# Selective scan: 512-column scans with a carried start value become 1024-column scans with a standing zero decay between the two halves

## The chip, the cores and the metric

The kernel runs on one core of a Trainium2 chip. The metric is the device time of one launch in microseconds (us); lower is better.

## The reference, cut to what matters

The reference is a chain of four layers on a tensor of 2 images with 128 channels of 64x64 pixels. Layers 0 to 2 (attention, a snake convolution, three convolution steps) are not touched. Layer 3 runs a Mamba block over each image in four directions (rows and columns, each forwards and backwards). Its core is a linear recurrence over 4096 positions, for 256 inner channels times 16 states:

```
dA = jnp.exp(dt[..., None] * A)
dBu = dt[..., None] * Bm[:, :, None, :] * xh[..., None]
def step(h, inp):
    dA_t, dBu_t = inp
    h = dA_t * h + dBu_t
    return (h, h)
_, hs = lax.scan(step, h0, (dA.transpose(1, 0, 2, 3), dBu.transpose(1, 0, 2, 3)))
y = jnp.einsum('lbdn,bln->bld', hs, Cm)
```

`dA` is the decay, `dBu` the input term (the "product with B"), `hs` the states, and `y` sums the states times C.

## The kernel before, in words

**Tiling.** Layer 3 (`layer3`, from line 1230) cuts each sequence of 4096 into 8 chunks of `BLK` = 512 positions. Two images, four directions and 8 chunks give 64 blocks. In a block the 256 x 16 states are worked off as 8 *groups* of 512 states: half `hf` (0, 1) by quarter of the states `ng` (0 to 3). The text calls them g0 to g7 (g0 to g3 are `hf` 0, g4 to g7 are `hf` 1). A group has a tile `db` of 128 partitions x 4 columns `q` x 512 positions, which holds first the product with B, then (in place) the states, then (in place) the states times C.

**The loop.** The main loop runs over the groups, k = 8i + slot, with the names "block i, slot s". The order on each engine is written by hand (`tc.manual_schedule()`), and every engine works off its own list in that order; between engines there are semaphores only. One turn of the loop with number k does:

- TensorE: `weights(k+2)` (line 1501), at the start of the turn: a matmul that spreads the four rows of B that this group needs over the partitions, into the PSUM tile `pbc` (pool `psb`, 2 buffers).
- ScalarE: `expo` (1544) computes one decay tile `da` of 512 columns (pool `psd`, 3 buffers of PSUM), two tiles ahead of the scan that uses it. For some columns it also runs an activation on a single column (1550) which adds the decayed last state of the previous chunk to the first product, so that the scan may start at 0.0. Those are columns q = 2, 3, and all four where VectorE makes no product; the other scans take the last state `hl` as their start value.
- VectorE: `scan` (1558) four times, 512 columns each; then `db_dve(k+1)` (1522), the product with B for the first `ND[hf][ng]` of the 512 positions, read from `pbc`.
- ScalarE: `keep(k-1)` (1563) saves the last states.
- GpSimd: `cmul(k-1)` (1568) multiplies states by C, and `db_pool(k+2)` (1531) makes the product with B for the positions from `ND` on, from copies of B in SBUF.
- TensorE: `sums(k-2)` (1574, 1576) folds the states into `y`; at `ng` 0 it first adds the direct term (1574).

`ND` is (512, 0, 176, 512) for `hf` 0 and (512, 512, 0, 512) for `hf` 1. So g1 and g6 have their product wholly from GpSimd, and g2 has 336 of 512 positions from it.

**The front of the next block** is spread over the slots of this one. At the end of each turn come `front_pe`, `front_act` and `front_pool`, and then `sums(k-2)`:

| slot | TensorE | ScalarE |
|---|---|---|
| 0 | `xproj` (1428) | `xproj_copy` (two copies, 1434, 1436) |
| 1 | `delta` (1455) | `softplus` of half 0 (1461 to 1464) |
| 2 | `sum_parts` of half 0 (1469) | `softplus` of half 1, `sum_copy` (1472) |
| 3 | `sum_parts` of half 1, `xproj_rest` (1446, 1447) | `sum_copy`, `rest_copy` (1450) |
| 4 | `zproj` (1416) | `zproj_silu` (1422, with two table loads) |
| 5 | `sums`, `project` of the block before (1593, 1595), then `conv` of half 0 (1404) | |
| 6 | `conv` of half 1 (1404) | `finish` of the block before (1601, 1603 or 1606) |
| 7 | | `conv_silu` (1409, with two table loads) |

All these TensorE results go through the PSUM pool `psm` with two buffers, so a matmul waits until the result two places earlier in that pool has been read. In slots 2 and 6 VectorE also gates `y` (1585). In 13 of the 64 blocks a layer norm of 512 columns for later use is spread over the same slots (`ln_mean` and others, lines 1326 to 1362).

The eight PSUM banks go to: `psd` 3, `psb` 2, `psy` 1 (for `y`), `psm` 2.

Of the kernel before, what the change touches and what calls it, by code (L numbers as in the profile page):

```python
# [1229 lines left out]
def layer3(g, I, out):  # L1230
# [5 lines left out]
    nc, tc = g.nc, g.tc  # L1236
    NJ = 4

    ND = ((BLK, 0, 176, BLK), (BLK, BLK, 0, BLK))
    NNG = N_STATE // NJ  # L1240
    HB = 1
    HC = 3
    with ExitStack() as ctx:
        a = ctx.enter_context(tc.tile_pool(name="l3a", bufs=1))
        dr = ctx.enter_context(tc.tile_pool(name="l3dr", bufs=2, space=bass.MemoryType.DRAM))
        psd = ctx.enter_context(tc.tile_pool(name="l3psd", bufs=3, space=PSUM))
        psb = ctx.enter_context(tc.tile_pool(name="l3psb", bufs=2, space=PSUM))
        psy = ctx.enter_context(tc.tile_pool(name="l3psy", bufs=1, space=PSUM))
        psm = ctx.enter_context(tc.tile_pool(name="l3psm", bufs=2, space=PSUM))

# [64 lines left out]
        xt = a.tile([P, L + 2 * HC], F32, name="xt")  # L1315
        N = {}
        NFIRST = 3


        def ln_tile():  # L1320

            return psd.tile([P, BLK], F32, name="da")

        def ln_mean(b, k):
            N[k, "mean"] = ln_tile()
            nc.tensor.matmul(N[k, "mean"], onesm, interior(g, b, k * RB, RB), start=True, stop=True)

        def ln_less(b, k):
# [10 lines left out]
            nc.scalar.activation(N[k, "sq"], N[k, "xc"], AF.Square)  # L1339

        def ln_var(b, k):
            N[k, "var"] = ln_tile()
            nc.tensor.matmul(N[k, "var"], onesm, N[k, "sq"], start=True, stop=True)


        def ln_log(b, k):
            nc.scalar.activation(N[k, "sq"], N[k, "var"], AF.Ln, bias=g.eps5)
# [37 lines left out]
        def reverse(i):  # L1385
            b, nd, _ = blocks[i]
            return dirs[b][nd][2]
# [91 lines left out]
        def spread_store(i, hf):  # L1479

            S[i]["dx", hf] = dr.tile([P, 2, BLK], F32, name="dx")
            nc.sync.dma_start(S[i]["dx", hf], S[i].pop(("dd", hf)))

        def spread_load(i, hf):
            s_ = S[i]
            dx = s_.pop(("dx", hf))
            dd4 = d4.tile([P, 2, 4, BLK], F32, name="dd4")
            for x in range(2):
                src = dx[:, x, :].rearrange("(q c) t -> c q t", c=32)
                for j in range(NJ):  # L1490
                    nc.sync.dma_start(dd4[32 * j : 32 * j + 32, x], src)
            s_["d4", hf] = dd4

        def weights(k):

            i, hf, ng = groups[k]
            G[k] = {}
            if ND[hf][ng] == 0:
                return
            pb = psb.tile([P, BLK], F32, name="pbc")  # L1500
            nc.tensor.matmul(pb, sel[:, ng].rearrange("p j c -> p (j c)"), S[i]["bc"], start=True, stop=True)  # L1501
            G[k]["pb"] = pb
# [8 lines left out]
                nc.sync.dma_start(t[32 * j : 32 * j + 32], S[i]["bx"][r0 + j].partition_broadcast(32))  # L1511

        def db_tile(k):
            if "db" not in G[k]:
                G[k]["db"] = wk.tile([P, 4, BLK], F32, name="db")
            return G[k]["db"]

        def db_dve(k):
            i, hf, ng = groups[k]
            n = ND[hf][ng]  # L1520
            if n:
                nc.vector.tensor_tensor(  # L1522
                    db_tile(k)[:, :, :n], G[k].pop("pb")[:, :n].unsqueeze(1).to_broadcast([P, 4, n]),
                    S[i]["d4", hf][:, 1, :, :n], ALU.mult,
                )
# [7 lines left out]
                    S[i]["d4", hf][:, 1, :, n:], ALU.mult,  # L1533
                )

        def carried(k, q):

            i, hf, ng = groups[k]
            return i % NBLK > 0 and (q >= 2 or ND[hf][ng] == 0)

        def expo(k, q):
            i, hf, ng = groups[k]
            da = psd.tile([P, BLK], F32, name="da")
            nc.scalar.activation(da, S[i]["d4", hf][:, 0, q, :], AF.Exp, scale=am[:, hf, q, ng : ng + 1])  # L1544
            G[k]["da", q] = da
            if carried(k, q):

                first = BLK - 1 if reverse(i) else 0
                b0 = G[k]["db"][:, q, first : first + 1]
                nc.scalar.activation(b0, da[:, first : first + 1], AF.Identity, bias=b0, scale=hl[:, hf, ng, q, :])  # L1550

        def scan(k, q):
            i, hf, ng = groups[k]
            d0, d1 = G[k].pop(("da", q)), G[k]["db"][:, q, :]
            if reverse(i):
                d0, d1 = d0[:, ::-1], d1[:, ::-1]
            zero = i % NBLK == 0 or carried(k, q)
            nc.vector.tensor_tensor_scan(d1, d0, d1, 0.0 if zero else hl[:, hf, ng, q, :], ALU.mult, ALU.add)  # L1558

        def keep(k):  # L1560
            i, hf, ng = groups[k]
# [75 lines left out]
        def transfers(i, slot):  # L1637
            if i < NBK:
                if slot == 1:
                    bc_store(i)  # L1640
                elif slot == 4:
                    spread_store(i, 0)
                elif slot == 5:
                    spread_load(i, 0)
                    spread_store(i, 1)
            if slot == 0 and i - 1 < NBK:
                spread_load(i - 1, 1)
            for x, ahead in (("b", 4), ("c", 1)):
                j, ng = divmod(8 * (i - 1) + slot + ahead, 8)
                if ng < NNG and 0 < j < NBK:  # L1650
                    copies(j, x, ng)
# [21 lines left out]
        def front_pool(i, slot):  # L1673
            if i < NBK:
                if slot in (3, 4):
                    spread(i, slot - 3)
# [9 lines left out]
        with tc.manual_schedule():  # L1686
# [4 lines left out]
            nc.vector.memset(xt[:, HC + L :], 0.0)  # L1691
            nc.vector.memset(xn[:, HB - 1, HW - HC :], 0.0)
            nc.vector.memset(xn[:, HB + HW, :HC], 0.0)
            units = [(k, q) for k in range(len(groups)) for q in range(4)]
            AHEAD = 2

            for k in range(NFIRST):
                ln_mean(0, k)
            for k in range(NFIRST):
# [34 lines left out]
            for ng in range(NNG):  # L1734
                copies(0, "b", ng)
                copies(0, "c", ng)
            for k in range(2):
                weights(k)
            db_dve(0)
            db_pool(0)  # L1740
            front_pe(0, 4)
            front_act(0, 4)
            front_pe(0, 5)
            front_pe(0, 6)
            for u in range(AHEAD):
                expo(*units[u])
            front_act(0, 7)
            db_pool(1)
            for k in range(len(groups) + 7):
                i, slot = divmod(k, 8)  # L1750
                live = k < len(groups)
                more = k + 1 < len(groups)
                ended = 1 <= k <= len(groups)
                transfers(i + 1, slot)
                if k + 2 < len(groups):
                    weights(k + 2)
                norm = next_norm(i)
                for q in range(4):
                    if slot == 6 and q == 3 and 1 <= i <= NBK:
                        finish(i - 1)  # L1760
                    if norm and slot == 2 and q == 3:
                        ln_log(*norm)
                    if q == 0 and ended:
                        keep(k - 1)
                    if 4 * k + q + AHEAD < len(units):
                        expo(*units[4 * k + q + AHEAD])
                    if norm and q == 0:
                        if slot == 0:
                            ln_mean(*norm)
                        elif slot == 2:  # L1770
                            ln_var(*norm)
                    if live:
                        scan(k, q)

                    for j, hf in (((k - 6) // 8, 0), ((k - 10) // 8, 1)):
                        if q == 1 and 8 * j + 6 + 4 * hf == k and 0 <= j < NBK:
                            gate(j, hf)
                if norm and slot == 0:
                    ln_less(*norm)
                if more:  # L1780
                    db_dve(k + 1)
                if ended:
                    cmul(k - 1)
                if k + 2 < len(groups):
                    db_pool(k + 2)

                if slot == 5 and 0 <= k - 2 < len(groups):
                    sums(k - 2)
                if slot == 5 and 1 <= i <= NBK:
                    project(i - 1)  # L1790
                front_pe(i + 1, slot)
                front_act(i + 1, slot)
                front_pool(i + 1, slot)
                if norm:
                    if slot == 1:
                        ln_square(*norm)
                    elif slot == 3:
                        ln_root(*norm)
                    elif slot == 5:
                        ln_scale(*norm)  # L1800
                    elif slot == 6:
                        ln_store(*norm)
                if live:

                    if slot == 6 and 0 < i % (4 * NBLK) <= NBLK // 2:
                        for n in range(2):
                            turn(blocks[i][0], 2 * (i % (4 * NBLK) - 1) + n)

                if slot != 5 and 0 <= k - 2 < len(groups):
                    sums(k - 2)  # L1810


@with_exitstack
# [157 lines left out]
```

## Time and profile before

| quantity | value |
|---|---|
| median of 3 runs | 5609.23 us (5607.43 to 5609.56) |
| the profiled execution's own time | 5610.11 us |
| its span, first to last instruction | 5608.3 us |
| first and last scan of layer 3 start at | 2309.3 and 5593.2 us |
| busy share of the span: TensorE, VectorE, ScalarE, GpSimd | 84%, 81%, 73%, 65% |
| mean granted TensorE clock | 0.877 |

The page of the profile gives busy time of each engine (PE is TensorE, PEld its weight loads, DVE is VectorE, ACT is ScalarE, POOL is GpSimd), groups of equal instructions with their busy time, the mean duration of one in ns and the idle time ahead of them with what ended it ("<-"). A timeline lists an engine's instructions in order: start in us, duration in us, engine, line, operation, output <- input, "x" the count of merged ones, and in brackets the idle time just before. Instructions of an engine overlap a little at their ends, so four of 1.20 us can take 4.57 us. Layer 3 is the stretch from 2309 us to the end: 64 blocks in some 3284 us, 51.3 us each.

### The profile page before, as it was taken

The numbers are of one execution on the slowest core, as the hardware profiler recorded it, in microseconds if no ns is written. First come the engines' busy times: TensorE is split into PE (matmuls) and PEld (weight loads), VectorE is DVE, ScalarE is ACT, GpSimd is POOL, SyncE is SP. The second block draws the span as 40 slices with busy tenths as digits, with TensorE's granted clock in tenths as the row PEclk, the third lists the DMA queues.
The fourth block names the chain that finished last, engine by engine and source line by source line (L and its number), as shares of the span: only waits on it lengthen the run. The fifth ranks groups of instructions, "written<-read, shape, count | busy, mean of one in ns | idle before, by whom it ended". The sixth has DMA issues, their size and how long they took to land.

```text
span 5608.3 us, 54471 instructions
## 1 busy us (share of the span) xinstructions
PE 4731.0 (84%) x17062; PEld 1757.8 (31%) x17062; DVE 4537.0 (81%) x4232; ACT 4086.5 (73%) x6282; POOL 3661.7 (65%) x1197
## 2 busy tenths in 40 slices
PE   6999999899788699777788887878888888877786
PEld 3444444344344244222222222222222222222221
DVE  6566555552144998699999999999999999999998
ACT  3999999500255311698888888888888888888886
POOL 6222222100100311599999999999999999999999
PEclk8999999999899899888888888888878787888887
DMA  4111111300375000465565556556555655565554
GB/s 155 38 46 46 31 31 38 62 1 1 76 128 83 27 0 0 104 143 129 129 141 137 135 126 144 129 129 148 140 133 128 144 134 131 130 147 131 134 137 106
DMA packets 334569, 554.27 MB, mean 99 GB/s; under 512 B 69264, under 2 KB 115872, under 8 KB 334080
## 3 DMA queue, kind: packets, MB, share of 16 engines
q1 hardware_dynamic: 331136, 547.17, 41.2%
q10 hardware_dynamic: 3136, 3.56, 0.3%
q8 instruction: 135, 2.21, 0.2%
q14 instruction: 162, 1.33, 0.1%
HBM read 461.40 MB, written 89.13 MB: 98 GB/s over the span
## 4 chain that ended last, share of the span: by engine, by line
DVE 45%; PE 35%; ACT 11%; issue 5%; DMA 2%; POOL 1%; SPq 1%; DVEq 0%; ACTq 0%; POOLq 0%
DVE db L1558 30%; DVE db L1522 11%; PE ps L312 8%; PE acc L328 8%; PE m L1112 5%; PE m L600 5%; ACT da L1544 4%; PE acd L846 2%; ACT db L1550 1%; DVE gt L1585 1%; PE m L560 1%; ACT L1409 1%; ACT u L1409 1%; PE pf L809 1%; DMA hats<-pos 1%
## 5 line engine op out<-in xcount | busy, mean ns | idle before, releaser
L1568 POOL TENSOR_TENSOR db<-db,c 128x2048 f32<-128x2048 f32 x512 | 2314.0, 4535 | 48.3 <-ACT hl L1563 32.7
L1544 ACT ACTIVATE da<-dd,am 128x512 f32<-128x512 f32 x2048 | 1398.6, 687 | 300.4 <-DVE db L1558 281.6
L1558 DVE TENSOR_TENSOR_SCAN db<-da,db 128x512 f32<-128x512 f32 x1376 | 1585.2, 1204 | 36.3 <-ACT db L1550 28.1
L318 ACT ACTIVATE e<-ps 128x1536 f16<-128x1536 f32 (+1 forms) x683 | 919.0, 1624 | 7.9 <-PE ps L312 7.9
L1558 DVE TENSOR_TENSOR_SCAN db<-da,hl,db 128x512 f32<-128x512 f32 x672 | 825.9, 1271 | 41.6 <-POOL db L1531 2.6
L1522 DVE TENSOR_TENSOR db<-pbc,dd 128x2048 f32<-128x2048 f32 (+1 forms) x384 | 781.3, 2035 | 32.1 <-DMA dd<-dx 32.1
L1531 POOL TENSOR_TENSOR db<-b,dd 128x2048 f32<-128x2048 f32 (+1 forms) x192 | 773.5, 4029 | 12.7 <-DMA b<-bx 12.7
L1576 PE MATMUL py<-db,fold 128*32 128x512 f32 x4096 | 615.6, 687 | 153.2 <-POOL db L1568 153.1
L312 PE MATMUL ps<-q 128*128 128x512 f16 x2048 | 554.0, 379 | 4.3 <-DVE flag L260 2.7
L328 PE MATMUL acc<-e,v 128*128 128x512 f16 x2048 | 553.7, 379 | 0.1
L346 POOL TENSOR_TENSOR parts<-parts 32x512 f32<-32x512 f32 x64 | 80.6, 1259 | 707.5 <-DVE parts L345 707.5
L1550 ACT ACTIVATE db<-da,db,hl 128x1 f32<-128x1 f32 x1120 | 394.0, 352 | 146.7 <-DVE db L1522 103.2
L339 DVE RECIPROCAL rec<-acc 32x512 f32<-32x512 f32 x64 | 214.9, 3358 | 257.9 <-PE acc L328 248.3
L1112 PE MATMUL m<-v,u 128*128 128x512 f32 x864 | 379.3, 602 | 41.8 <-DVE v L1055 40.9
L1469 PE MATMUL pm<-dd,ident 128*128 128x512 f32 x512 | 359.7, 841 | 2.5 <-ACT dd L1462 2.5
L1428 PE MATMUL pm<-u,wxp 128*72 128x512 f32 x256 | 196.7, 913 | 141.0 <-ACT u L1409 141.0
L1501 PE MATMUL pbc<-bc,sel 64*128 64x512 f32 x384 | 208.3, 542 | 123.6 <-DVE db L1522 122.8
L312 PEld LDWEIGHTS <-q 128*128 128x128 f16 x2048 | 197.7, 97 | 278.5 <-issue 103.6
L328 PEld LDWEIGHTS <-v 128*128 128x128 bf16 x2048 | 199.3, 97 | 248.8 <-issue 10.2
L600 PE MATMUL m<-comb,w 64*128 64x512 f32 (+4 forms) x1296 | 269.9, 575 | 0.0
L720 POOL TENSOR_SCALAR yt<-y 32x512 f32<-32x512 f32 x8 | 18.1, 2268 | 380.8 <-DVE y L711 380.4
L1576 PEld LDWEIGHTS py<-db,fold 128*32 128x32 f32 x4096 | 90.6, 114 | 553.2 <-issue 306.7
(324 smaller groups left out, 6563.4 us busy)
## 6 DMA issues: line engine op xcount, KB each, us to landing
dd<-dx SPq DMA_DIRECT2D x1024, 256.0 KB, 6.5
dx<-dd SPq DMA_DIRECT2D x128, 512.0 KB, 5.4
c<-bx SPq DMA_DIRECT2D x1024, 64.0 KB, 2.1
hats<-pos SPq DMA_DIRECT2D x136, 256.0 KB, 9.8
b<-bx SPq DMA_DIRECT2D x512, 64.0 KB, 4.6
piece<-qd SPq DMA_DIRECT2D x128, 128.0 KB, 2.8
piece<-kd SPq DMA_DIRECT2D x112, 128.0 KB, 2.7
w<-in_conv0T SPq DMA_DIRECT2D x18, 288.0 KB, 8.5
```

The lines of the kernel that those rows point to most:

```text
L312: nc.tensor.matmul(ps[:, i, :], t[:, 1, kb * P : (kb + 1) * P], t[:, 0, qb * BLK : (qb + 1) * BLK], start=True, stop=True,)
L318: nc.scalar.activation(e[:, :n, :], ps[:, :n, :], AF.Exp, scale=1.0 / UP**2)
L328: nc.tensor.matmul(acc, v3[b][:, kb, h, :], e[:, i, :], start=(kb == 0), stop=(kb == NS - 1))
L600: yield lambda q=q, dy=dy, src=src, i0=i0, i1=i1: nc.tensor.matmul(m[:, i0 * NF : i1 * NF], w[half, dy, q, x, :], src, start=(dy == KC and ...
L1112: nc.tensor.matmul(m[x], weights[j][:, dy, x, :], v[j][b][:, x, r0 : r0 + RP, :].rearrange("p r i -> p (r i)"), start=(dy == 0), stop=(dy ...
L1522: nc.vector.tensor_tensor(db_tile(k)[:, :, :n], G[k].pop("pb")[:, :n].unsqueeze(1).to_broadcast([P, 4, n]), S[i]["d4", hf][:, 1, :, :n], A ...
L1531: nc.gpsimd.tensor_tensor(db_tile(k)[:, :, n:], S[i]["b", ng][:, n:].unsqueeze(1).to_broadcast([P, 4, BLK - n]), S[i]["d4", hf][:, 1, :, n ...
L1544: nc.scalar.activation(da, S[i]["d4", hf][:, 0, q, :], AF.Exp, scale=am[:, hf, q, ng : ng + 1])
L1550: nc.scalar.activation(b0, da[:, first : first + 1], AF.Identity, bias=b0, scale=hl[:, hf, ng, q, :])
L1558: nc.vector.tensor_tensor_scan(d1, d0, d1, 0.0 if zero else hl[:, hf, ng, q, :], ALU.mult, ALU.add)
L1568: nc.gpsimd.tensor_mul(v, v, S[i]["c", ng].unsqueeze(1).to_broadcast([P, 4, BLK]))
L1576: nc.tensor.matmul(S[i]["y", hf][32 * q : 32 * q + 32, :], fold, G[k]["db"][:, q, :], start=False, stop=(ng == NNG - 1),)
```

## The change

Two 512-column decays now stand side by side in one PSUM tile of 1024 columns; there are two such tiles, `decays[0]` for q = 0, 1 and `decays[1]` for q = 2, 3, and one scan runs over each. At the border between the halves one decay column stands at zero, so that the second half starts afresh: `border` sets it with a memset when the direction of the scan changes, and `expo` leaves it out.

Since no scan has a start value now, the last state of the previous chunk is added to the first product in every column: `carry` runs four single-column activations per group. The decay of the first position that it needs comes from a small side path: `first_load` (DMA) fetches the first `dt` column, `first_decays` (GpSimd) multiplies it by A, `first_exp` (ScalarE) takes the exponential.

The four decays of PSUM take four banks, so `psb` goes from 2 buffers to 1, and `weights(k+2)` moves from the start of a turn to its very end, after `front_pe` and `sums(k-2)`. The product `db_dve(k+1)` moves from after the four scans to between the two. `keep(k)` moves into the turn of its group, after the second scan. Decays for group k+1 are computed after each scan of group k has freed its tile. `finish` and `ln_log` of slots 6 and 2 move behind the second pair of exponentials. The layer norm's means and variances of later blocks take buffers of `psm`. `ND[0][2]` goes from 176 to 384.

```
-    ND = ((BLK, 0, 176, BLK), (BLK, BLK, 0, BLK))
+    ND = ((BLK, 0, 384, BLK), (BLK, BLK, 0, BLK))
...
-        psd = ctx.enter_context(tc.tile_pool(name="l3psd", bufs=3, space=PSUM))
-        psb = ctx.enter_context(tc.tile_pool(name="l3psb", bufs=2, space=PSUM))
+        psd = ctx.enter_context(tc.tile_pool(name="l3psd", bufs=1, space=PSUM))
+        psb = ctx.enter_context(tc.tile_pool(name="l3psb", bufs=1, space=PSUM))
...
+        decays = [psd.tile([P, 2, BLK], F32, name=f"da{p}") for p in range(2)]
+
+        def ln_tile(b, k):
+            if b == 0 and k < NFIRST:
+                return decays[k // 2][:, k % 2, :]
+            return psm.tile([P, BLK], F32, name="pm3")
...
+        def first_load(i, hf):
+            if i % NBLK:
+                first = BLK - 1 if reverse(i) else 0
+                src = S[i]["dx", hf][:, 0, first : first + 1].rearrange("(q c) t -> c (q t)", c=32)
+                df = S[i]["df", hf] = ck.tile([P, 4], F32, name=f"df{hf}")
+                for j in range(NJ):
+                    nc.sync.dma_start(df[32 * j : 32 * j + 32], src)
+
+        def first_decays(i, hf):
+            if i % NBLK:
+                e = S[i]["e", hf] = ck.tile([P, NNG, 4], F32, name=f"e{hf}")
+                nc.gpsimd.tensor_tensor(
+                    e, S[i].pop(("df", hf)).unsqueeze(1).to_broadcast([P, NNG, 4]),
+                    am[:, hf].rearrange("p q n -> p n q"), ALU.mult,
+                )
+
+        def first_exp(i, hf):
+            if i % NBLK:
+                nc.scalar.activation(S[i]["e", hf], S[i]["e", hf], AF.Exp)
+
+        def carry(k):
+            i, hf, ng = groups[k]
+            if i % NBLK:
+                first = BLK - 1 if reverse(i) else 0
+                for q in range(4):
+                    b0 = G[k]["db"][:, q, first : first + 1]
+                    nc.scalar.activation(
+                        b0, S[i]["e", hf][:, ng, q : q + 1], AF.Identity, bias=b0, scale=hl[:, hf, ng, q, :]
+                    )
...
+        def border(p, rev):
+            x = BLK - 1 if rev else 0
+            nc.vector.memset(decays[p][:, 0 if rev else 1, x : x + 1], 0.0)
+
+        def expo(k, p):
             i, hf, ng = groups[k]
+            rev = reverse(i)
+            if k == 0 or reverse(groups[k - 1][0]) != rev:
+                border(p, rev)
+            for x in range(2):
+                r = slice(0, BLK)
+                if rev and x == 0:
+                    r = slice(0, BLK - 1)
+                elif not rev and x == 1:
+                    r = slice(1, BLK)
+                q = 2 * p + x
+                nc.scalar.activation(
+                    decays[p][:, x, r], S[i]["d4", hf][:, 0, q, r], AF.Exp, scale=am[:, hf, q, ng : ng + 1]
+                )
+
+        def scan(k, p):
+            i, hf, ng = groups[k]
+            d0 = decays[p].rearrange("p x t -> p (x t)")
+            d1 = G[k]["db"][:, 2 * p : 2 * p + 2, :].rearrange("p x t -> p (x t)")
             if reverse(i):
                 d0, d1 = d0[:, ::-1], d1[:, ::-1]
-            zero = i % NBLK == 0 or carried(k, q)
-            nc.vector.tensor_tensor_scan(d1, d0, d1, 0.0 if zero else hl[:, hf, ng, q, :], ALU.mult, ALU.add)
+            nc.vector.tensor_tensor_scan(d1, d0, d1, 0.0, ALU.mult, ALU.add)
...
                 elif slot == 5:
+                    first_load(i, 0)
                     spread_load(i, 0)
                     spread_store(i, 1)
+                elif slot == 6:
+                    first_load(i, 1)
...
                 transfers(i + 1, slot)
-                if k + 2 < len(groups):
-                    weights(k + 2)
                 norm = next_norm(i)
...
+                by_vector = more and ND[groups[k + 1][1]][groups[k + 1][2]] > 0
+                if more and not by_vector:
+                    carry(k + 1)
+                if live:
+                    scan(k, 0)
+                if more:
+                    db_dve(k + 1)
+                    expo(k + 1, 0)
+                if slot == 7 and more:
+                    first_exp(i + 1, 0)
+                elif slot == 2 and live:
+                    first_exp(i, 1)
+                if by_vector:
+                    carry(k + 1)
+                for j, hf in (((k - 6) // 8, 0), ((k - 10) // 8, 1)):
+                    if 8 * j + 6 + 4 * hf == k and 0 <= j < NBK:
+                        gate(j, hf)
+                if live:
+                    scan(k, 1)
+                    keep(k)
+                if more:
+                    expo(k + 1, 1)
+                if slot == 6 and 1 <= i <= NBK:
+                    finish(i - 1)
...
                 front_pe(i + 1, slot)
                 front_act(i + 1, slot)
                 front_pool(i + 1, slot)
+                if slot == 6 and i + 1 < NBK:
+                    first_decays(i + 1, 0)
+                elif slot == 1 and live:
+                    first_decays(i, 1)
...
                 if slot != 5 and 0 <= k - 2 < len(groups):
                     sums(k - 2)
+                if k + 2 < len(groups):
+                    weights(k + 2)
```

## The prediction on record

> **What bounds the kernel now.** I read the windows of the trace first, then the groups, then the timelines of VectorE, TensorE and ScalarE over one block. The windows (columns: time, PE, PEld, DVE, ACT, POOL busy, TensorE clock, DMA share, GB/s):
>
> ```profile
> 3000.00:3500.00 500.00, 410.73 (x1188) 126.93 (x1186) 488.88 (x392) 422.96 (x780) 491.33 (x128) 0.82 0.58 137
> 4000.00:4500.00 500.00, 418.20 (x1193) 127.94 (x1191) 488.89 (x392) 428.64 (x787) 493.56 (x128) 0.80 0.56 134
> ```
>
> In layer 3 VectorE (98%) and GpSimd (98 to 99%) are both full, ScalarE is at 85%, TensorE at 82%. So a block of 51.3 us is set by the work of the two full engines, and the other two keep ahead of them. The groups give the prices:
>
> ```profile
> L1568 POOL TENSOR_TENSOR db<-db,c 128x2048 f32<-128x2048 f32 x512 | 2314.0, 4535 | 48.3 <-ACT hl L1563 32.7
> L1558 DVE TENSOR_TENSOR_SCAN db<-da,db 128x512 f32<-128x512 f32 x1376 | 1585.2, 1204 | 36.3 <-ACT db L1550 28.1
> L1558 DVE TENSOR_TENSOR_SCAN db<-da,hl,db 128x512 f32<-128x512 f32 x672 | 825.9, 1271 | 41.6 <-POOL db L1531 2.6
> ```
>
> Idle time of VectorE at its scans is small: 36 and 42 us in all. No product of VectorE waits for TensorE. VectorE's timeline shows what one costs in a row:
>
> ```profile
> 4026.05 2.33 DVE L1558 TENSOR_TENSOR_SCAN db<-da,db 128x512 f32<-128x512 f32 x2
> 4028.29 2.27 DVE L1522 TENSOR_TENSOR db<-pbc,dd 128x2048 f32<-128x2048 f32 x1
> 4030.67 2.46 DVE L1558 TENSOR_TENSOR_SCAN db<-da,hl,db 128x512 f32<-128x512 f32 x2
> 4033.04 2.31 DVE L1558 TENSOR_TENSOR_SCAN db<-da,db 128x512 f32<-128x512 f32 x2
> ```
>
> A pair of scans from 0.0 takes 2.24 us start to start, with a start value 2.37, and after a product there is a gap of 0.1. Last, how TensorE keeps ahead (slots 0 and 2, then 5 and 6):
>
> ```profile
> 4011.75 3.63 PE L1428 MATMUL pm<-u,wxp 128*72 128x512 f32 x4 [2.77 <-ACT u L1409]
> ...
> 4023.73 3.78 PE L1469 MATMUL pm<-dd,ident 128*128 128x512 f32 x4
> 4027.31 1.83 PE L1574 MATMUL py<-u,ddp 128*128 128x512 f32 x2
> 4029.07 1.06 PE L1576 MATMUL py<-db,fold 128*32 128x512 f32 x8
> ...
> 4043.91 2.26 PE L1593 MATMUL pm<-xa,ident 128*128 128x512 f32 x2 [1.44 <-ACT z L1422]
> 4045.99 3.57 PE L1595 MATMUL pm<-gt,mt 128*128 128x512 f32 x4
> 4049.38 3.62 PE L1404 MATMUL pm<-xt,wcs 128*128 128x512 f32 x8
> 4052.92 0.49 PE L1501 MATMUL pbc<-bc,sel 64*128 64x512 f32 x1
> 4053.59 3.70 PE L1404 MATMUL pm<-xt,wcs 128*128 128x512 f32 x8 [0.18 <-ACT xa L1601]
> ```
>
> TensorE waits for ScalarE's silu (L1409, L1422) and for `finish` (L1601), then runs long strings. Today the small matmul L1501 stands ahead of the string of its turn, with over a turn to spare. ScalarE, around slot 7 to 0:
>
> ```profile
> 4009.72 1.28 ACT L1409 ACT_TABLE_LOAD   x1
> 4011.01 1.27 ACT L1409 ACTIVATE u<-pm,vecs 128x512 f32<-128x512 f32 x2
> 4012.30 1.28 ACT L1410 ACT_TABLE_LOAD   x1
> ...
> 4014.41 0.35 ACT L1550 ACTIVATE db<-da,db,hl 128x1 f32<-128x1 f32 x1
> 4014.66 0.68 ACT L1544 ACTIVATE da<-dd,am 128x512 f32<-128x512 f32 x1
> ...
> 4020.67 1.29 ACT L1544 ACTIVATE da<-dd,am 128x512 f32<-128x512 f32 x2
> ```
>
> The silu with its two table loads is 3.87 us in which no decay is made; two decays take 1.29; the next instruction follows a one-column one after 0.25.
>
> **What the Trainium skill says.** "ScalarE: Activation LUTs", section What ACT_TABLE_LOAD costs: a load is about 1283 ns (here 1.28), each pointer operand of an activation adds about 93 ns, and activations in a row overlap by about 93. The one-column one has two pointers: 0.35 here, and 0.35 - 0.09 agrees with 0.25. "TensorE: Matmul & The Clock Gate", section What's actually happening: after an idle window of about 3.4 us the array runs at half clock until it has been busy as long. The trace agrees: 0.9 us each for L1428 after 2.77 us of idling, 0.45 each for L1404 after a busy spell. "PSUM — Partial Sum Buffer", section Engine vs sequencer instructions: VectorE's, ScalarE's and GpSimd's queues are strict first in, first out; so a waiting product holds back the scan behind it.
>
> **Part by part, per block.**
> *Scans.* 32 go, 16 come. A 1024-column scan isn't in the trace. From a product of 704 columns (0.87 us) and one of 2048 (2.27) VectorE's fixed part is 0.13; so a 512 scan is 0.13 + 512 x 2.09 ns, and 1024 take 2.27, or 2.19 start to start. Ends: 2.10 and 2.30. With 12 scans that had a start value, before: 10 x 2.24 + 6 x 2.37 = 36.6; after 16 x 2.19 = 35.0: -1.6.
> *ND 384.* 208 x 4 more product columns on VectorE at 1.04 ns: +0.9. Off GpSimd: from its 3012 ns at 1344 and 4512 at 2048, 2.13 ns x 832 = -1.8. VectorE's list is then 35.0 + 5 x 2.37 + 1.84 + two gates 1.16 = 49.9, and GpSimd's, with two tiny multiplies (below), about 49.5. That is what could be gained.
> *Tiny side path.* `first_decays`: 2 on GpSimd, 16 columns: 0.2 to 0.3 each from its fixed part (4512 - 2048 x 2.13 = 150 ns), behind it `cmul`s that will have slack. `first_exp` 0.2 twice on ScalarE, behind the exponentials, beside the product of 2.27. `first_load`: 8 more issues on SP at 0.47 (8 of `dd<-dx` take 3.8), and its wait for the store; behind it `spread_load`, 1.9 us later, and the B copies. Needed in slot 7, two turns later: hidden. Its transfer of 4-byte pieces isn't shown: if it lasted as long as a `dd` load (6.5 us), still hidden; beyond about 10 us it would delay slot 7. I take 0. `border`: a memset of 0.06 at a change of direction: nothing.
> *Carry.* 32 one-column activations instead of 20, with 1.05 (4 x 0.25, overlapped) to 1.41 us (4 x 0.35) per group; I take 1.05. They lie beside the product, except ahead of g1 and g6, which have none.
> *Sums of ScalarE* rise from 44 to about 46 to 48 us per block. It would fit, were it not for the order.
>
> **The moved wait.** `weights(k+2)` is now last in turn k, behind `front_pe` and `sums`, and its product is asked for after the first scan of turn k+1; behind that product on VectorE stands the second scan, and behind that scan ScalarE's `keep` and decays, and the front that TensorE waits for. The lead was over a turn (6.4 us); it is now one scan (2.2) against strings of 4 to 10 us. I walk one block along what ends last, from the product of g7 (in slot 6) round to the next. A hand-over to ScalarE with `keep` is 0.15.
> (A) to the product of the next g0 (slot 7): product and gap 2.37, gate 0.58, scan 2.27, keep 0.15, two decays 1.29, `finish` 0.88 (mean of 0.95, 0.99, 0.58), conv, which needs the buffer that `finish` frees, 5.3, direct term and fold 2.0, weights 0.5, hand-over 0.05: **15.4**. TensorE has idled 7 us ahead of this conv, so half of it is cold: 3.4 us of 0.9, the rest of 0.45. Ends 3.6 (warm) and 7.2 (cold).
> (B) to g1's first scan: product 2.37, scan 2.27, 0.15, decays 1.29, silu with loads 3.87, carry 1.05, decays 1.29, 0.05: **12.3**.
> (C) to g4's product (slot 3): scan 2.2, product of 1536 columns 1.84, scan 2.27, 0.15, decays 1.29, softplus 2.52, `sum_parts` 3.6, direct term and fold 2.8, weights 0.55: **17.2**.
> (D) to g7's product: product 2.37, scans 2.2 + 2.2, product 2.37, scan 2.27, 0.15, decays 1.29, table 1.28, first silu 0.6, project 5.5, conv 3.55 (warm behind it), weights 0.55: **24.3**.
> Sum **69.3**. The 13 norm blocks: `ln_var` takes one more `psm` buffer in slot 2, and `sum_parts` then waits for the softplus of the same turn: 6.5 x 13/64 = +1.3. The 8 blocks without a carry: -0.1. So 70.5 against 51.3: 64 x 19.2 = +1228. From the profiled 5610.1 (span 5608.3 and 1.8 around it): **6838 us**; the median shown is 0.9 below the profiled time, which doesn't matter here. VectorE's work is some 50 of the 70.5: it idles about 20, of which 12.5 at L1522's products for TensorE (8.0 at g0, 3.1 at g7, 1.4 at g4) and 6.5 at g1's and g6's scans for ScalarE. Where the stall of before goes: nowhere, it was under 1 us.
>
> **Rivals.**
> *Only ScalarE ties.* If the matmul comes in time after all (TensorE at 60% has room), the stalls left are those at g1 and g6: ScalarE has 3.87 or 3.65 us of silu, then carry and decays, while VectorE has two scans: 3.3 + 3.1 on 49.9 = 56.3 per block, +5.0 x 64: 5930 us. Against: the strings don't depend on how loaded TensorE is.
> *The sums decide (faster).* Place: VectorE's list. Price: 49.9 + 0.6 of stalls against 51.3: -0.85 x 64 = 5556 us. It decides if weights and decays are there when asked, so from strings under 2.2 us and a front of ScalarE under 0.5 us ahead of g1 and g6. For it: both full engines lose 0.7 to 1.3 us. Against: 3.62 for a conv alone, 3.87 for the silu.
> *All cold.* With every matmul at half clock (conv and fold in D too) and carries at 0.35: +5 on 69.3, about 7150.
>
> **How the numbers follow.** Chains as walked 0.67, ScalarE only 0.16, faster 0.12, all cold 0.03, no change 0.02. The likeliest alone: conv warm -1.7, scans and carries short -1, some slack that I don't see -2; conv cold +1.9: 6550 to 7000. The range must leave out no more than 0.2, so it takes in the second case: 5900 to 7000. Slower 0.86, same 0.02, faster 0.12; 0.2% is about what a measurement of this kernel can tell from no change.
>
> **What would show it.** L1522's successor with idle time "<-PE pbc" of some 800 us, scans idle for ScalarE some 400; scan of 2.27; VectorE at about 72% in layer 3, GpSimd about 70%; TensorE's clock under 0.8. Wrong if products don't wait for `pbc`, or if TensorE's list isn't in written order.

## The result and the profile after

The changed kernel takes 6735.32 us (median of 6 runs, 6733.45 to 6738.83) against 5609.4 us before (6 runs): a ratio of 1.2008, 95% interval 1.1993 to 1.2024. The forecast was 6838 us, so the direction and the mechanism held, and the size was 103 us too high. The profiled execution took 6734.19 us, with a span of 6732.4.

The windows of layer 3 (columns as before: time, PE, PEld, DVE, ACT, POOL busy, TensorE clock, DMA share, GB/s):

```profile
3000.00:3500.00 500.00, 322.38 (x894) 95.56 (x892) 360.83 (x178) 339.60 (x668) 359.12 (x109) 0.75 0.43 100
5000.00:5500.00 500.00, 326.71 (x897) 97.96 (x896) 361.54 (x178) 342.45 (x673) 364.79 (x110) 0.75 0.44 104
```

No engine is full any more: VectorE 72%, GpSimd 72 to 73%, ScalarE 68%, TensorE 65%. Where before two engines were full, here the engines wait for each other in turn. The groups of the changed kernel say for whom:

```profile
L1607 POOL TENSOR_TENSOR db<-db,c 128x2048 f32<-128x2048 f32 x512 | 2316.3, 4528 | 873.3 <-ACT hl L1602 750.1
L1597 DVE TENSOR_TENSOR_SCAN db<-da,db 128x1024 f32<-128x1024 f32 x1024 | 2286.4, 2274 | 412.7 <-ACT da L1586 412.5
L1554 DVE TENSOR_TENSOR db<-pbc,dd 128x2048 f32<-128x2048 f32 (+1 forms) x384 | 841.4, 2191 | 849.7 <-PE pbc L1533 817.1
L1522 ACT ACTIVATE db<-e,db,hl 128x1 f32<-128x1 f32 x1792 | 545.8, 376 | 746.6 <-DVE db L1554 743.1
```

The scan of 1024 columns takes 2274 ns. VectorE's busy time over all went down from 4537.0 to 4494.5 us. But it idles 817 us at products for the weights matmul L1533 and 412 us at scans for ScalarE's decays, 1230 us together; the loss is 1126. ScalarE in its turn waits 743 us for the product (its carry stands behind it), and GpSimd 750 us for ScalarE's `keep`.

VectorE's timeline over one plain block (no norm), from g0's product to the next g0's:

```profile
4969.19 2.29 DVE L1554 TENSOR_TENSOR db<-pbc,dd 128x2048 f32<-128x2048 f32 x1 [8.91 <-PE pbc L1533]
...
4981.74 2.29 DVE L1597 TENSOR_TENSOR_SCAN db<-da,db 128x1024 f32<-128x1024 f32 x1 [3.70 <-ACT da L1586]
...
4997.69 2.29 DVE L1554 TENSOR_TENSOR db<-pbc,dd 128x2048 f32<-128x2048 f32 x1 [0.47 <-PE pbc L1533]
...
5016.62 2.29 DVE L1597 TENSOR_TENSOR_SCAN db<-da,db 128x1024 f32<-128x1024 f32 x1 [3.52 <-ACT da L1586]
5021.27 2.29 DVE L1554 TENSOR_TENSOR db<-pbc,dd 128x2048 f32<-128x2048 f32 x1 [2.36 <-PE pbc L1533]
...
5037.46 2.29 DVE L1554 TENSOR_TENSOR db<-pbc,dd 128x2048 f32<-128x2048 f32 x1 [8.92 <-PE pbc L1533]
```

Ahead of the lines with a bracket VectorE waits: for g0's product (first line), g1's scan, g4's product, g6's scan, g7's product, and the next g0's product. From one g0 to the next are 68.27 us, of which 3.70 + 0.47 + 3.52 + 2.36 + 8.92 = 18.97 are waits. TensorE in the stretch ahead of the last two of these, g7's and g0's products (conv is L1405, weights L1533):

```profile
5012.24 2.16 PE L1632 MATMUL pm<-xa,ident 128*128 128x512 f32 x2 [4.09 <-ACT z L1423]
5014.23 3.15 PE L1634 MATMUL pm<-gt,mt 128*128 128x512 f32 x4
5017.21 3.60 PE L1405 MATMUL pm<-xt,wcs 128*128 128x512 f32 x8
5020.74 0.49 PE L1533 MATMUL pbc<-bc,sel 64*128 64x512 f32 x1
5029.09 6.05 PE L1405 MATMUL pm<-xt,wcs 128*128 128x512 f32 x8 [7.86 <-ACT xa L1640]
5034.98 1.02 PE L1613 MATMUL py<-u,ddp 128*128 128x512 f32 x2
5035.93 1.06 PE L1615 MATMUL py<-db,fold 128*32 128x512 f32 x8
5036.93 0.49 PE L1533 MATMUL pbc<-bc,sel 64*128 64x512 f32 x1
```

Each weights matmul (0.49) stands behind its string, and the product on VectorE starts 0.04 us after it. TensorE itself idles 7.86 us ahead of the second conv, for `finish` (L1640). ScalarE's list over the same stretch shows why `finish` is late:

```profile
5023.60 1.22 ACT L1522 ACTIVATE db<-e,db,hl 128x1 f32<-128x1 f32 x4 [3.24 <-DVE db L1554]
5026.39 0.20 ACT L1602 COPY hl<-db 128x4 f32<-128x4 f32 x1 [1.57 <-DVE db L1597]
5026.49 1.41 ACT L1586 ACTIVATE da<-dd,am 128x512 f32<-128x512 f32 x2
5027.84 1.20 ACT L1640 ACTIVATE xa<-pm,vecs 128x512 f32<-128x512 f32 x1
```

`finish` stands behind `keep` and g7's decays, these wait for VectorE's second scan of g6, and that scan stands behind g7's product. That is the ring of the prediction. ScalarE idles 3.24 us ahead of the carry (L1522) in the same turn, which is where e1 below puts `finish`.

### The profile page after: what moved, and what is told of

The parts are those of the page before. It is cut to its first block, busy times and chain, and to the rows that moved or that the text cites. A ratio compares the mean times of both kernels' runs of the same rounds, so it can differ in the third digit from the quotient of the medians.

```text
span 6732.4 us, 54677 instructions
## 1 busy us (share of the span) xinstructions
PE 4923.0 (73%) x17062; PEld 1801.5 (27%) x17062; DVE 4494.5 (67%) x3220; ACT 4309.5 (64%) x7066; POOL 3579.8 (53%) x1309
## 3 DMA queue, kind: packets, MB, share of 16 engines
q8 instruction: 135, 2.21, 0.1%
## 4 chain that ended last, share of the span: by engine, by line
PE 51%; DVE 24%; ACT 14%; issue 6%; DMA 2%; POOL 2%; SPq 1%; ACTq 0%; POOLq 0%; DVEq 0%
DVE db L1597 12%; DVE db L1554 10%; PE pm L1405 9%; PE ps L312 7%; PE acc L328 7%; ACT da L1586 5%; PE m L1112 5%; PE m L600 4%; PE pm L1470 3%; PE pm L1634 2%; PE py L1615 2%; PE py L1613 2%; PE pm L1632 2%; PE acd L846 1%; PE pbc L1533 1%
## 5 line engine op out<-in xcount | busy, mean ns | idle before, releaser
L1597 DVE TENSOR_TENSOR_SCAN db<-da,db 128x1024 f32<-128x1024 f32 x1024 | 2286.4, 2274 | 412.7 <-ACT da L1586 412.5
L1586 ACT ACTIVATE da<-dd,am 128x512 f32<-128x512 f32 (+1 forms) x2048 | 1409.2, 688 | 166.8 <-DVE db L1597 68.6
L1554 DVE TENSOR_TENSOR db<-pbc,dd 128x2048 f32<-128x2048 f32 (+1 forms) x384 | 841.4, 2191 | 849.7 <-PE pbc L1533 817.1
L1522 ACT ACTIVATE db<-e,db,hl 128x1 f32<-128x1 f32 x1792 | 545.8, 376 | 746.6 <-DVE db L1554 743.1
L1563 POOL TENSOR_TENSOR db<-b,dd 128x2048 f32<-128x2048 f32 (+1 forms) x192 | 659.9, 3437 | 374.7 <-DMA dd<-dx 242.8
L1470 PE MATMUL pm<-dd,ident 128*128 128x512 f32 x512 | 375.9, 857 | 268.1 <-ACT dd L1463 223.7
L1405 PE MATMUL pm<-xt,wcs 128*128 128x512 f32 x512 | 314.9, 772 | 246.6 <-ACT xa L1642 139.9
L1429 PE MATMUL pm<-u,wxp 128*72 128x512 f32 x256 | 231.8, 1059 | 356.7 <-ACT u L1410 356.7
L1405 PE MATMUL pm<-xn,wcs 128*128 128x512 f32 x512 | 321.9, 786 | 217.8 <-ACT xa L1642 104.7
L1602 ACT COPY hl<-db 128x4 f32<-128x4 f32 x512 | 98.8, 193 | 471.8 <-DVE db L1597 470.6
L1632 PE MATMUL pm<-xa,ident 128*128 128x512 f32 x128 | 124.4, 1064 | 254.8 <-ACT z L1423 254.8
```

Of the source, the lines that this page charges most:

```text
L1405: nc.tensor.matmul(pu, wcs[:, hf, s, :], window(blk, sgn * s), start=(s == 0), stop=(s == 3))
L1470: nc.tensor.matmul(ps, g.ident, S[i]["dd", hf][:, x, :], start=(x == 0), stop=(x == 1))
L1554: nc.vector.tensor_tensor(db_tile(k)[:, :, :n], G[k].pop("pb")[:, :n].unsqueeze(1).to_broadcast([P, 4, n]), S[i]["d4", hf][:, 1, :, :n], A ...
L1563: nc.gpsimd.tensor_tensor(db_tile(k)[:, :, n:], S[i]["b", ng][:, n:].unsqueeze(1).to_broadcast([P, 4, BLK - n]), S[i]["d4", hf][:, 1, :, n ...
L1586: nc.scalar.activation(decays[p][:, x, r], S[i]["d4", hf][:, 0, q, r], AF.Exp, scale=am[:, hf, q, ng : ng + 1])
L1597: nc.vector.tensor_tensor_scan(d1, d0, d1, 0.0, ALU.mult, ALU.add)
```

## The experiments

Each edit is to the changed kernel unless it says "the kernel before". Each was timed beside the kernel before on its own chip: e1 to e4 on one chip, e5 to e8 on a second, e9 and e10 on a third.

| run | us | ratio to before, 95% |
|---|---|---|
| e1: finish early | 6136.44 | 1.0923 to 1.0960 |
| e2: weights early | 6082.5 | 1.0829 to 1.0865 |
| e3: before, ND 384 | 5659.91 | 1.0078 to 1.0112 |
| e4: before, weights late | 5607.47 | 0.9992 to 1.0010 |
| e5: finish and weights early | 5934.16 | 1.0563 to 1.0598 |
| e6: e5, groups swapped | 5659.78 | 1.0076 to 1.0109 |
| e7: e6, half carry | 5610.99 | 0.9998 to 1.0016 |
| e8: e7, norm moved | 5578.3 | 0.9931 to 0.9964 |
| e9: e8, ND 304 | 5568.47 | 0.9912 to 0.9939 |
| e10: e9, mixed carry | 5567.19 | 0.9906 to 0.9934 |

**e1, finish ahead of the carry in slot 6.**

```
+                if slot == 6 and 1 <= i <= NBK:
+                    finish(i - 1)
                 if by_vector:
                     carry(k + 1)
...
                 if more:
                     expo(k + 1, 1)
-                if slot == 6 and 1 <= i <= NBK:
-                    finish(i - 1)
```

> The changed kernel, with finish moved from behind the second pair of exponentials of slot 6 to ahead of that turn's carry, where ScalarE idles. Theory (the chain from finish over conv and sums to g0's weights holds back g0's product): conv can start behind g7's weights at once and finds the array warm; g0's weights come before the product is asked for, its wait falls from 9.0 us to under 1, the block from 68.4 to some 59.5 us: about 6165 us. Rival (the array at half clock is what costs, not the place in the list): conv gets warm and saves 3 us per block: about 6545 us. Rival (ScalarE alone ties the block): no change, 6735.

Measured 6136, the theory's number within 30 us. One instruction per block, moved by a few places on an engine with idle time, is worth 599 us. TensorE in e1:

```profile
4425.21 0.49 PE L1533 MATMUL pbc<-bc,sel 64*128 64x512 f32 x1
4426.60 3.70 PE L1405 MATMUL pm<-xt,wcs 128*128 128x512 f32 x8 [0.90 <-ACT xa L1640]
4430.14 1.02 PE L1613 MATMUL py<-u,ddp 128*128 128x512 f32 x2
4431.09 1.07 PE L1615 MATMUL py<-db,fold 128*32 128x512 f32 x8
4432.09 0.49 PE L1533 MATMUL pbc<-bc,sel 64*128 64x512 f32 x1
```

The wait ahead of the conv is 0.90 us instead of 7.86, and the conv takes 3.70 instead of 6.05: the array has stayed warm. The clock alone is worth 2.4 us of the 9.4 by which a block got shorter, so the rival that put all on the clock is out; ScalarE alone is out too. VectorE's waits at products fell from 817.1 to 222.7 us; those at scans stayed at 412.5.

**e2, weights directly behind the product of their turn.**

```
                 if more:
                     db_dve(k + 1)
+                if k + 2 < len(groups):
+                    weights(k + 2)
+                if more:
                     expo(k + 1, 0)
...
-                if k + 2 < len(groups):
-                    weights(k + 2)
```

> The changed kernel, with weights(k+2) directly behind the product db_dve(k+1) of its turn in the written order, so ahead of front_pe and sums on TensorE, still with one buffer. Theory: no product waits for weights any more (817 us before), the stalls at g1's and g6's scans for ScalarE stay at about 400 us; 56.3 us per block: about 5930 us. Rival: TensorE, now waiting in mid-turn for the one buffer, delivers the front later, and the stall moves to ScalarE and its decays: above 6165 us.

Measured 6082: neither's number. No product waits for weights any more, as the theory said, but the waits at scans grew. VectorE's waits in e2:

```profile
DVE db L1597 <- ACT da L1586: 505.0, 115, 7.8
DVE db L1597 <- POOL db L1607: 41.6, 11, 3.8
DVE db L1597 <- ACT db L1522: 31.7, 29, 2.0
```

The late `finish` still makes the conv late and cold. In e2's trace the conv runs 6.74 us from 4440.05; its `sums` come behind it; GpSimd gets its next `db` tile late; and ScalarE's carry for g1 then waits 3.12 us for GpSimd's product. So the theory was wrong to let nothing but the weights hang on that string: buffers hang on it too. e5, which differs from e2 in the place of `finish` alone, confirms it.

**e5, both moves.**

> The changed kernel with both moves: finish ahead of the carry of slot 6, weights(k+2) directly behind the product of its turn. Theory: what e1 still lost at products (223 us) and what e2 lost behind a late finish (a cold conv, then late sums and late buffers) both go; only ScalarE's ties at g1 and g6 are left, 3.5 + 3.7 us per block: about 56.5 us per block, 5920 us. Rival: the one buffer of the weights holds TensorE in mid-turn and brings back stalls elsewhere: above 6000 us.

Measured 5934, the theory's number within 15 us: the plain block is 56.18 us. `psb` still has its one buffer, TensorE idles 421 us in all for it, and yet no product of VectorE waits for weights: the lost buffer by itself doesn't cost the time, the place of the weights in the list does. This is the case that the prediction had as its rival "only ScalarE ties" (56.3 per block, 5930 us); it is what is left when the ties through TensorE's matmuls are taken out. VectorE's first wait in e5:

```profile
DVE db L1597 <- ACT da L1586: 400.9, 128, 3.9
```

That is two waits per block (128 in 64 blocks) of some 3.1 us on average, at g1 and g6.

**e6, other groups without a product on VectorE.**

```
-    ND = ((BLK, 0, 384, BLK), (BLK, BLK, 0, BLK))
+    ND = ((BLK, BLK, 0, 384), (BLK, BLK, BLK, 0))
```

> As the run with both moves, and ND is ((512, 512, 0, 384), (512, 512, 512, 0)): the groups without a product on VectorE are g2 and g7, no longer g1 and g6, which follow the two silus of ScalarE; amounts of work are the same. Theory (a silu ahead of a turn without a product ties the block): the stalls of 7.2 us per block go but for some 1 to 2 us behind the silus: about 51 us per block, 5560 to 5640 us. Rival (ScalarE's sum of work, over 46 us with its waits, ties wherever it stands): less than half of it goes, above 5780 us.

Measured 5660, some 20 us over the theory's band and 120 short of the rival's: the theory's reason holds, and its estimate of what is left was a little low. The plain block is 51.67 us. Amounts of work are equal, only the places of the two groups without a product and of the group with 384 columns are other: 274 us. Of the 7.2 us per block that were to go, 4.5 went and 2.7 are left, not 1 to 2. VectorE's waits at scans in e6:

```profile
DVE db L1597 <- ACT db L1522: 117.6, 132, 2.0
...
DVE db L1597 <- ACT da L1586: 67.8, 68, 7.7
```

**e7, half the carry.**

```
-                for q in range(4):
+                for q in (0, 2) if reverse(i) else (1, 3):
...
-            nc.vector.tensor_tensor_scan(d1, d0, d1, 0.0, ALU.mult, ALU.add)
+            h0 = hl[:, hf, ng, 2 * p + (1 if reverse(i) else 0), :] if i % NBLK else 0.0
+            nc.vector.tensor_tensor_scan(d1, d0, d1, h0, ALU.mult, ALU.add)
```

> As the run with groups swapped, but the carry covers only the second half of each scan (two columns per group instead of four); the first half takes the last state as the scan's start value, as the kernel before does. ScalarE loses 0.6 us per group, VectorE gains 0.07 us per scan. Theory (VectorE's list sets the block once the ties are gone): slower than the swapped run by up to 1.1 us per block, some 60 us. Rival (ScalarE's ties still set it): faster by up to 60 us.

Measured 5611, 49 us faster than e6: the rival is right, ScalarE's ties were still the bound. VectorE in layer 3 is now 98% busy, though each scan with a start value takes 2337 ns instead of 2274.

**e8, the norm's variance from slot 2 to 3.**

```
-                elif norm and slot == 2:
+                elif norm and slot == 3:
                     ln_var(*norm)
...
                 if by_vector:
                     carry(k + 1)
+                if norm and slot == 3:
+                    ln_log(*norm)
...
-                if norm and slot == 2:
-                    ln_log(*norm)
```

> As the run with the half carry, and in the 13 norm blocks ln_var moves from slot 2 to slot 3 and ln_log with it, ahead of keep. Theory (ln_var's extra buffer makes sum_parts wait for the softplus of the same turn, so ScalarE waits for TensorE): these blocks lose their excess of 3 to 4 us, some 45 us in all against the half-carry run. Rival (the excess is the norm's own work on ScalarE and VectorE): no change within 10 us.

Measured 5578, 33 us faster than e7: norm blocks fall from between 52.4 and 54.3 to between 50.4 and 51.5 us, plain ones stay at 50.88. So most of the excess was a wait. The edit moves two things at once, `ln_var` with its buffer and `ln_log`, and the run doesn't part them. What held `sum_parts` back was not the softplus, as the expectation has it: in the changed kernel's trace it starts at 2539.60, right behind `ln_log` (2538.88, 0.67 us), which reads the buffer that `ln_var` took.

**e3, the kernel before with ND 384 alone.**

```
-    ND = ((BLK, 0, 176, BLK), (BLK, BLK, 0, BLK))
+    ND = ((BLK, 0, 384, BLK), (BLK, BLK, 0, BLK))
```

> The kernel before with ND[0][2] at 384 alone. By the sums of work: VectorE +0.87 us per block, GpSimd -1.77 us. Theory (VectorE as full as GpSimd): slower by 0.5 to 0.9 us per block, 5640 to 5665 us. Rival (GpSimd sets the block): faster, down to 5560 us.

Measured 5660, as the theory says: VectorE's list, not GpSimd's, sets the block in the kernel before. This part alone costs 52 us there.

**e4, the kernel before with weights at the end of the turn.**

```
                 transfers(i + 1, slot)
-                if k + 2 < len(groups):
-                    weights(k + 2)
...
                 if slot != 5 and 0 <= k - 2 < len(groups):
                     sums(k - 2)
+                if k + 2 < len(groups):
+                    weights(k + 2)
```

> The kernel before with weights(k+2) at the end of its turn, both buffers and the old 512-column scans kept, product still behind all four scans. Theory (the strings of TensorE ahead of the weights decide, and only the lead changes): the lead is a whole turn here, so stalls only at g7 (about 3 us) and g0 (about 1 us), none at the others: about 5865 us. Rival (a late place harms only with the product between the scans): within 10 us of 5609.

(A line that makes a group's table entry when it is first asked for is left out.)

Measured 5607, no change: my theory's number was wrong by 258 us, and the rival's number is right. TensorE in e4, slots 6 and 7, and the product that VectorE then makes:

```profile
4402.47 0.49 PE L1501 MATMUL pbc<-bc,sel 64*128 64x512 f32 x1
4403.35 3.70 PE L1404 MATMUL pm<-xt,wcs 128*128 128x512 f32 x8 [0.39 <-ACT xa L1601]
4406.89 1.02 PE L1574 MATMUL py<-u,ddp 128*128 128x512 f32 x2
4407.84 1.07 PE L1576 MATMUL py<-db,fold 128*32 128x512 f32 x8
4408.84 0.49 PE L1501 MATMUL pbc<-bc,sel 64*128 64x512 f32 x1
```

```profile
4411.03 2.27 DVE L1522 TENSOR_TENSOR db<-pbc,dd 128x2048 f32<-128x2048 f32 x1
```

The weights end at 4409.33, the product starts at 4411.03: 1.7 us to spare. In the old order `finish` runs between the exponentials of its turn (4402.10 in this trace) and the product is asked for after four scans instead of one. So the late place of the matmul is harmless by itself, with both buffers and the old scans. With the new order it is not: e1 and e5, both with `finish` early, differ in the place of the weights alone, by 202 us. Of what sets the two orders apart, the early place of the product is the likely partner: asked for after the first pair of scans, at about 4408.8 in this trace, it would already have waited some 0.5 us (an estimate from these lines and from 2.24 us for a pair). The early product on its own, in the kernel before, was not run.

**e9, ND 304.** The edit is `384` to `304` in e8's ND.

> As the run with the norm moved, with ND[0][3] at 304 instead of 384. In that run VectorE is busy 98.5% and GpSimd 97%. 80 x 4 product columns move from VectorE (-0.33 us per block) to GpSimd (+0.68 us). Theory (VectorE's list sets the block now, as the sums of work say): 0.3 us per block faster, about 5558 us. Rival (GpSimd's lag ties through the five db tiles): no faster, or slower by up to 25 us.

Measured 5568.47 against 5578.3 on another chip: 10 us, or some 13 when each is set against the kernel before on its own chip, where 20 were expected. In the traces the plain block falls from 50.88 to 50.55 us, which is the theory's step. But of the 63 times from block to block 38 are the plain one in e8 and 27 in e9, and the norm blocks gain next to nothing (51.0 and 50.9 us on average). GpSimd, full again, may be what holds these; that is not shown. A window of e8, then of e9:

```profile
4500.00:5000.00 500.00, 383.42 (x1198) 118.81 (x1192) 491.98 (x240) 418.82 (x772) 483.16 (x147) 0.86 0.59 137
```

```profile
4500.00:5000.00 500.00, 395.07 (x1208) 121.28 (x1206) 490.90 (x241) 418.63 (x777) 491.74 (x148) 0.86 0.60 136
```

VectorE and GpSimd are both at 98% again, GpSimd up from 97%.

**e10, full carry for g0, g3, g5 and g7.**

```
+    FULL = (0, 3, 5, 7)
...
-                for q in (0, 2) if reverse(i) else (1, 3):
+                for q in range(4) if k % 8 in FULL else (0, 2) if reverse(i) else (1, 3):
...
-            h0 = hl[:, hf, ng, 2 * p + (1 if reverse(i) else 0), :] if i % NBLK else 0.0
+            h0 = hl[:, hf, ng, 2 * p + (1 if reverse(i) else 0), :] if i % NBLK and k % 8 not in FULL else 0.0
```

> As the run with ND 304, and g0, g3, g5 and g7, ahead of whose scans ScalarE idles, take the full carry of four columns and scans from 0.0; the other four groups keep the half carry. VectorE loses 8 x 0.07 us per block. Theory (VectorE's list): 0.5 us per block faster than that run, some 30 us. Rival (ScalarE's idle time there isn't free, or GpSimd is the bound by now): no faster.

Measured 5567.19, the same as e9 within the noise: the rival is right. The same window:

```profile
4500.00:5000.00 500.00, 396.10 (x1206) 123.56 (x1198) 488.98 (x241) 439.64 (x849) 492.75 (x148) 0.86 0.60 137
```

VectorE does less, GpSimd as much as in e9, the time stays. The plain block did fall, from 50.55 to 50.30 us, half of the theory's step, but only 15 of the 63 are plain now. Which of the rival's two reasons holds the others back is not shown. The best version, e9 or e10, is 0.6 to 0.9% faster than the kernel before.

## Why the prediction was right, point by point

- **What bounds the kernel before**: right in part. VectorE and GpSimd are both full, but e3 shows that it is VectorE's sum that sets the block.
- **Scan of 1024**: 2.27 us forecast, 2274 ns measured.
- **The moved wait decides**: right. Waits at products 817 us (800 forecast), at scans 412 (about 400). By place, in the plain block: g0 8.9 (8.0), g7 2.4 (3.1), g4 0.5 (1.4), scans of g1 and g6 3.70 + 3.52 (3.3 + 3.1).
- **The four parts of the ring**, forecast and measured between the starts shown above: (A) 15.4 and 16.2; (B) 12.3 and 12.55; (C) 17.2 and 15.95; (D) 24.3 and 23.6. Sum 69.3 and 68.27. A and B came out 1.0 us longer than forecast and C and D 2.0 shorter; that these partly cancel is luck.
- **Terms mis-sized in A**: the conv was taken as half cold, 5.3 us, and took 6.05 here: the clock stayed at half for 4.8 us of it, not 3.4 (last section). `finish` was taken at 0.88, a mean of its three forms, and took 1.20. Over the kernel the mean of one of the conv's matmuls is 772 to 786 ns, against 602 before.
- **Term mis-sized in C**: I had `sum_parts` begin after the whole softplus. It begins after the second of its four activations; in the trace the matmul L1470 starts at 4990.66, when L1463 ends, 1.2 us ahead of the softplus's end at 4991.88. So C is 1.25 shorter, and g4's product hardly waits.
- **Term mis-sized in D**: `project` was taken at 5.5 and took 4.97 (5012.24 to 5017.21).
- **The gap of 0.1 us between a product and a scan** is gone: in the changed kernel the scan starts 2.21 us after the start of the product (4969.19 to 4971.40), not 2.38. The forecast carried it five times in the ring.
- **Carry**: 1.05 forecast for four, 1.22 measured (one is 376 ns instead of 352).
- **Norm blocks**: 6.5 us more each forecast; about 75.0 against 68.3 measured. The size was right, but the wait was named wrongly: `sum_parts` waits for `ln_log`, not for the softplus of its turn. That the size came out all the same is luck.
- **The reading of the clock**: the prediction says that the trace agrees with an idle window of about 3.4 us ahead of half clock. It doesn't quite: L1428 ran at 0.9 us per matmul after only 2.77 us of idling. The idling of 7 us in A is long by either measure.
- **Costed at nothing**: `df` loads land in 1.6 us; no other engine waits for `first_decays` (0.21 to 0.25 us each). The border's memset (59 ns, 12 times) has ScalarE wait 63 us in 6 places. In the written order it stands behind g0's product, which itself waits for weights there, so I see no time of its own for it; it was not tried apart.
- **The 103 us too much**: 1.03 us x 64 = 66 from the sum of the ring. The first and the last time from one block to the next are short (62.1 and 54.5 us, where I took all 64 alike), another 20. The remaining 17 are not split.
- **Rivals**: "only ScalarE ties" is what e5 shows when the matmul ties are out. "The sums decide" is what e8 to e10 reach, after three more edits. "All cold" came near in the conv of A (6.05 of its 7.2), but the conv and the fold behind it were warm (3.60 in D, 1.06 in A). What was argued against the first rival in the prediction, that strings don't depend on TensorE's load, holds; but e4 shows that a string's length alone says nothing: what counts is how long before its product the weights can start, and when the product is asked for.

## What to carry to other kernels

A long instruction saves its fixed part per piece (here scans went from 2411 to 2286 us of busy time, 1.9 us per block; some 45 of these 125 us are the start value that 672 scans no longer take, at 67 ns each), but it also halves the number of places where something else can stand between, and a lead of a turn can become a lead of one instruction. Before merging, write down for every wait who is asked, when, and what stands ahead of it in its list; follow the path until it comes back to its start, and if that ring is longer than the work of the busiest engine, its length is the new time, whatever the busy shares are (here 68.3 us against some 50). When a ring is found, look for the member that could run earlier for free: here one activation, in an idle stretch of its engine, gave back 599 of 1126 us.

## What the runs showed of the hardware that I had not expected

In the changed kernel TensorE idles 7.2 to 7.9 us ahead of the conv of half 1, and from the second block on this string of eight matmuls takes 6.0 to 6.8 us with a granted clock of 0.54 to 0.61 on average. In the block shown the clock was 0.50 from 5029.1 to 5032.1 us and 0.71 from there to 5035.1: it stayed at half for 4.8 us of the 6.05. Over the blocks that time is 4.8 to 6.2 us. After 0.9 us of idling the same conv took 3.70 us (e1). "TensorE: Matmul & The Clock Gate", section What's actually happening in the Trainium skill, gives about 3.4 us of busy time for warming up and calls the window in which it is counted free-running; these traces show that it can take up to 1.8 times as long. In e2, after nearly the same idling in all blocks but two (4.3 to 5.0 us), the conv takes anything from 5.1 to 6.8 us, which fits a window that runs on its own.

A scan with a start value from SBUF costs 62 to 66 ns more than one from 0.0 at 1024 columns (2336 to 2340 against 2274, e7 to e10), about as at 512 (1271 and 1204): the operand's price doesn't grow with length.
